# One core, a four-layer network: zero rows put into spent tiles, expert outputs written image by image with the next layer's first tokens between them

## The chip, the cores and the metric

The kernel runs on one core of a Trainium2 chip. The metric is the device time of one execution in microseconds (us); the number shown is the median of several runs. The core's engines are named as in the profile: PE (TensorE's matmuls), PEld (its weight loads), DVE (VectorE), ACT (ScalarE), POOL (GpSimd) and SP (SyncE, which here issues most of the transfers).

## The reference, cut to what matters

Two images of 64 x 64 tokens with 128 channels pass through four layers, each an attention or mixing step and a feed-forward step, in float32. The change lies between the feed-forward step of layer 2 (64 experts, each of which takes its own 8 tokens of an image) and the attention of layer 3:

```python
# layer 2, experts; x is the normalized input, 4096 tokens per image
probs = jax.nn.softmax(x @ gate_w.T + gate_b, axis=1)      # over the tokens
vals, idx = jax.lax.top_k(probs.transpose(0, 2, 1), 8)     # 8 tokens per expert
pooled = jnp.einsum('bked,bke->bed', gathered, topv)       # [2, 64, 128]
h = gelu(pooled @ weight1[e, :128] + weight1[e, 128])      # [2, 512] for each expert
out = h @ weight2[e, :512] + weight2[e, 512]               # [2, 128] for each expert
outputs = outputs.at[image, idx].add(out * topv)           # back to the chosen tokens
t = t + outputs
# layer 3, attention; x is the layer norm of t
q, k, v = x @ Wq.T + bq, x @ Wk.T + bk, x @ Wv.T + bv
t = t + softmax(q @ k.T / sqrt(256)) @ v
```

## The kernel before, in words

The tokens `x` stay in SBUF the whole time as [128 partitions, 64 blocks, 128 channels]: 32 blocks of 128 tokens per image. A framework places every tile, derives all semaphore waits, and fixes each engine's order of instructions ahead of the run: by the order in the program, with later instructions drawn forward where an engine would stand idle in its plan. Each engine then works strictly in its order. The instructions inside a conditional block are kept together: nothing of theirs is drawn ahead of the branch.

`layer2_ffn` holds the experts of layer 2. Expert rows of both images sit on 128 partitions: image 0 on 0 to 63, image 1 on 64 to 127. Its steps are these.

- `weights(1, e)` loads the first weights in 16 pieces of 1 MB (four experts each) from SP's queue into the pool `ws`, which has 12 places. The piece `e` gives its place up after the matmuls that read it.
- The gate's probabilities `pr` [128, 4096] are finished: exponential, sum, the top 8 of each row. What is not chosen becomes zero. `rest` is a tile of 16 KB per partition for this, and `prT`, in the same place afterwards, holds the transposed probabilities.
- `f2pp` sums the chosen tokens of each expert. `st1` holds the result as windows: each expert's two columns (one per image) stand at the start of a window of 34 columns, and zeros follow, so that a slice of 32 columns has only this expert's columns in its own place and zeros elsewhere. These zeros are cleared by POOL once, in L1657.
- `f2ph` (L1710) multiplies by the first weights, four column groups side by side. The result gets its bias and the gelu and is transposed.
- `st2`, four tiles like `st1` (one for each 128 of the 512 hidden units), take four places of `ws`, are cleared by POOL (L1720), and get the hidden values by four copies (L1731).
- `weights(2, e)` loads the second weights in 16 pieces of 1 MB into the same 12 places. `f2po` (L1739) multiplies by them as the pieces come, 32 column-group matmuls a piece in the records.
- The result is put in order by a small matmul (`f2sort`), and `f2y` (L1769) brings it back to the tokens: for each of eight steps `g`, four blocks of each image, alternating between the images. A block's weights are the 64 rows of its image in `pr`. Two PSUM tiles a step, out of three, and two additions to `x` (L1778) follow.

After that `layer3` makes its pool: the expert weights `ew` (SP, 512 KB), the biases `eb` (cleared by POOL, four small loads by SP) and two small cleared tiles; and it branches on `w["small"]`, a bound on the scores that was computed in layer 2. With these inputs the branch `l3_bounded` runs. `l3_qkv(b, g)` prepares a group of four blocks: statistics and reciprocal root (`l3_stats`, with a square root on ACT), normalization into `v`, four transposes and a copy into `kT`, a matmul by the combined query-key weights into `qT`, and the value bias added to `x` by POOL. The loop then goes through query blocks of 512 tokens and pairs of key blocks `k2`: scores `sc` (L2126, `scl` in the profile), exponential, and, one pair later, the values `oT` (L2085) and a running sum `acc` on DVE. Group 0 is finished before the first scores; the groups 1 to 7 of image 0 are cut into pieces, two of which follow each pair of the first query block, so that group `g` is ready at pair `2 g`.

Of the kernel before, what the change touches and what calls it, by code (L numbers as in the profile page):

```python
# [8 lines left out]
F32 = mybir.dt.float32  # L9
AF = mybir.ActivationFunctionType  # L10
ALU = mybir.AluOpType
AX = mybir.AxisListType
PSUM = bass.MemoryType.PSUM

P = 128
B = 2
S = 64
L = S * S
NC = L // P
C = 128  # L20
# [3 lines left out]
E1 = 64  # L24
FF = 512
E2 = 8
# [13 lines left out]
class Net:  # L40
# [1084 lines left out]
        yield  # L1125


    def layer2(self, kept, done, w3):
        nc, tc, ins = self.nc, self.tc, self.ins
        with tc.tile_pool(reuse_waits="tile", name="g2", bufs=1) as gp:  # L1130
            with tc.tile_pool(reuse_waits="tile", name="g2p", bufs=1, space=PSUM) as ps:
                gwT = self.load_T(gp, ps, "gwT", ins["L2_ffn_gate_w"], E1, C)
            gb = gp.tile([P, 1], F32, tag="gb", name="f2gb")
            for b in range(B):
                rows = slice(b * E1, (b + 1) * E1)
                nc.sync.dma_start(out=gb[rows], in_=column(ins["L2_ffn_gate_b"]))


            pr = gp.tile([P, L], F32, tag="pr", name="f2pr")
            mx = gp.tile([P, NC // 4], F32, tag="mx", name="f2mx")  # L1140
            mv = gp.tile([P, B * NC, 2], F32, tag="mv", name="f2mv")
            r = gp.tile([P, B * NC], F32, tag="r", name="f2r")
            gate = gwT, gb, pr, mx, mv, r
            self.layer2_attn(gate, kept, w3)
            done()
            self.layer2_ffn(gate)

    def layer2_attn(self, gate, kept, w3):

# [470 lines left out]
                pass  # L1620


    def layer2_ffn(self, gate):

# [1 line left out]
        nc, tc, ins = self.nc, self.tc, self.ins  # L1628
        NT, NR, NF = 4, E1 // 4, FF // P
        WIN = 2 * NR + 2  # L1630
        with ExitStack() as st:
            wp = st.enter_context(tc.tile_pool(reuse_waits="tile", name="f2w", bufs=1))
            ap = st.enter_context(tc.tile_pool(reuse_waits="tile", name="f2a", bufs=1))
            ps = st.enter_context(tc.tile_pool(reuse_waits="tile", name="f2p", bufs=3, space=PSUM))
            ws = st.enter_context(tc.tile_pool(reuse_waits="tile", name="f2s", bufs=12))
            _, _, pr, mx, mv, r = gate

            def weights(kind, e):
# [17 lines left out]
            st1 = wp.tile([P, NT, NR, WIN], F32, tag="st1", name="f2st1")  # L1656
# [15 lines left out]
            nc.vector.tensor_scalar(pr, pr, sm, None, ALU.mult)  # L1672
            m8 = self.small.tile([P, 8], F32, tag="m8", name="f2m8")
            nc.vector.max(m8, pr)
            rest = ap.tile([P, L], F32, tag="rest", name="f2rest")
            nc.vector.match_replace(out=rest, in_to_replace=m8, in_values=pr, imm_value=0.0)
            nc.vector.tensor_tensor(pr, pr, rest, ALU.subtract)


            prT = ap.tile([P, NC, P], F32, tag="rest", name="f2prT")  # L1680
            for g in range(NC // 4):
                pt = ps.tile([P, 4, P], F32, tag="misc", name=f"f2prT{g}")
                for i in range(4):
                    n = 4 * g + i
# [23 lines left out]
            for e in range(NR):  # L1708
                for j in range(NT):
# [4 lines left out]
                        start=(e == 0),  # L1714
                        stop=(e == NR - 1),
                    )
            st2 = []
            for c in range(NF):
                s2 = ws.tile([P, NT, NR, WIN], F32, tag="w", name=f"f2st2_{c}")
                nc.gpsimd.memset(s2, 0.0)  # L1720
                st2.append(s2)
            w2 = [weights(2, e) for e in range(NR)]
            hid = wp.tile([P, FF], F32, tag="hid", name="f2hid")
            nc.vector.tensor_tensor(hid, ph, b1, ALU.add)
# [32 lines left out]
            eo = wp.tile([P, C], F32, tag="eob", name="f2eob")  # L1757
            nc.scalar.copy(eo, pt)


            for g in range(NC // 4):
                pts = [
                    ps.tile([P, 4, C], F32, tag="misc", name=f"f2y{b}_{g}") for b in range(B)
                ]
                for i in range(4):
                    n = 4 * g + i
                    for b in range(B):
                        rows = slice(b * E1, (b + 1) * E1)
                        nc.tensor.matmul(  # L1769
                            pts[b][:, i, :],  # L1770
                            lhsT=pr[rows, n * P : (n + 1) * P],
                            rhs=eo[rows, :],
                            start=True,
                            stop=True,
                        )
                for b in range(B):
                    xs = self.x[:, b * NC + 4 * g : b * NC + 4 * g + 4, :]
                    nc.vector.tensor_tensor(xs, xs, pts[b], ALU.add)  # L1778


    def layers(self):
# [9 lines left out]
        with tc.tile_pool(reuse_waits="tile", name="l3w", bufs=1, side="right") as wp:  # L1791
# [9 lines left out]
            w["bqk"] = wp.tile([P, 1], F32, tag="bqk", name="l3bqk")  # L1801
            space = self.layer1(xT, gst, na, nb, xp, kp)
            first.close()
            self.layer2(space, kept.close, w)
            self.layer3(w)

    def layer3(self, weights):
        nc, tc, ins = self.nc, self.tc, self.ins
        G = B * NC
        with ExitStack() as st:  # L1810
            wp = st.enter_context(tc.tile_pool(reuse_waits="tile", name="l3e", bufs=1))
            weights["ones"] = wp.tile([P, 1], F32, tag="ones", name="l3ones")
            nc.vector.memset(weights["ones"], 1.0)
            weights["ew"] = self.load(
                wp, "ew", [P, E2, C], ins["L3_ffn_expert_w"].rearrange("e d c -> d e c")
            )

            eb = weights["eb"] = wp.tile([P, 4, C], F32, tag="eb", name="f3eb")
            nc.gpsimd.memset(eb, 0.0)
            for i in range(4):  # L1820
                nc.sync.dma_start(
                    out=eb[32 * i : 32 * i + E2, i, :], in_=ins["L3_ffn_expert_b"]
                )


            self.xnT = wp.tile([P, B, L], F32, tag="xnT", name="f3xnT")
            self.lg = wp.tile([P, G, E2], F32, tag="lg", name="f3lg")
            self.wt = wp.tile([P, G, E2], F32, tag="wt", name="f3wt")
            weights["pads"] = []
            for i in range(2):  # L1830
                pad = wp.tile([P, 4, 32], F32, tag=f"pad{i}", name=f"f3pad{i}")
                nc.gpsimd.memset(pad, 0.0)
                weights["pads"].append(pad)
            with tc.If(weights["small"] > 0) as fits:
                self.l3_bounded(weights)
            with fits.Else():
                self.l3_any(weights)
            self.l3_experts(weights)

    def l3_weights(self, ap, ps, w, take):  # L1840

# [172 lines left out]
    def l3_bounded(self, w):  # L2014
# [7 lines left out]
        with (  # L2022
            tc.tile_pool(reuse_waits="tile", name="l3ba", bufs=2) as ap,
            tc.tile_pool(reuse_waits="tile", name="l3bp", bufs=2, space=PSUM) as ps,
        ):
            qT = ap.tile([P, L], F32, tag="qT", name="l3qT", bufs=1)
            kTs = [ap.tile([P, L], F32, tag="kT", name=f"l3kT{b}") for b in range(B)]
            vs = [ap.tile([P, NC, C], F32, tag="v", name=f"l3v{b}") for b in range(B)]
            jobs = {}

            def piece():
# [79 lines left out]
                        for g4 in range(NB, 2 * NB - 1):  # L2111
                            jobs["bias", g4] = self.f3_bias(ap, ps, w, g4, "f3f")

            for g in range(NB):
                jobs["keys", 0, g] = keys(0, g)
            for b in range(B):
                for qb in range(NB):
# [32 lines left out]
    def l3_any(self, w):  # L2150
# [3 lines left out]
        with (  # L2154
# [1 line left out]
            tc.tile_pool(reuse_waits="tile", name="l3ap", bufs=2, space=PSUM) as ps,  # L2156
        ):
            for b in range(B):
                qT = ap.tile([P, L], F32, tag="qT", name=f"l3aqT{b}")
                kT = ap.tile([P, L], F32, tag="kT", name=f"l3akT{b}")  # L2160
                v = ap.tile([P, NC, C], F32, tag="v", name=f"l3av{b}")
                for g in range(NB):
                    for _ in self.l3_qkv(ap, ps, w, b, g, qT, kT, v, "l3a"):
                        pass
                for q in range(NC):
# [138 lines left out]
```

## Time and profile before

The median of 4 runs is 4788.3 us (4787.81 to 4790.6). The profile shows one further execution.

| | us |
|---|---|
| the profiled execution's own time | 4788.73 |
| its span, first to last instruction | 4786.9 |
| PE busy | 4471.8 (93%) |
| DVE busy | 2944.1 (62%) |
| ACT busy | 2695.8 (56%) |
| POOL busy | 945.6 (20%) |
| POOL waits for `f2ph` before it clears `st2` (one wait) | 47.9 |
| DVE waits for `f2po` (one wait) | 41.7 |
| PE waits for loads of `f2w` in `f2po` (15 waits) | 12.4 |
| PE waits for the first normalized group of layer 3 (one wait) | 5.9 |

Idle time counts only on the engine that sets the end. The long waits of POOL and DVE belong to engines that had nothing else to do in that stage; PE's short waits lie on the engine that is busy for 93% of the span. The table of shares is an average over layers of quite different kinds, so a stage has to be read by its own stretch of time: the experts of layer 2 fill about 3550 to 3682 us, and the attention of layer 3 begins there and lasts to about 4656 us.

### The profile page before, as it was taken

The page shows a single profiled execution, that of the slowest core. Times are in us where ns is not written, and L with a number is a line of the kernel's source. Part 1 is how long each engine was busy: PE and PEld are TensorE (multiplying, and loading weights), DVE is VectorE, ACT ScalarE, POOL GpSimd, SP SyncE. Part 2 cuts the span into 40 slices and gives each one's busy share as a digit, 9 for nine tenths or more (in the row PEclk, how much of TensorE's full clock was granted, in tenths as well). Part 3 has the DMA queues.
Part 4 walks back from the last instruction along what each step waited for, and adds up shares of the span by engine and source line. Part 5 has one row for each costly group of instructions (what it writes and reads, how often), then busy time and mean ns, then how long its engine had stood idle before and what let it go on. Part 6 is the DMA issues. An engine that isn't in the chain of part 4 may idle for free.

```text
span 4786.9 us, 76270 instructions
## 1 busy us (share of the span) xinstructions
PE 4471.8 (93%) x32236; PEld 1742.8 (36%) x32236; DVE 2944.1 (62%) x4850; ACT 2695.8 (56%) x3157; POOL 945.6 (20%) x848
## 2 busy tenths in 40 slices
PE   6999999998999999977899999999967999999999
PEld 3333333333333333335323223223225444444444
DVE  5676767677766767766755657555554444444447
ACT  5666565666666665545666766676731444333326
POOL 1000000000000000004455555555521000000008
PEclk8999999999999999988999999999977999999999
DMA  1000000000000000000000000000034000000001
GB/s 47 10 1 10 1 10 1 10 1 1 10 1 10 1 13 1 1 5 21 6 1 1 1 1 1 1 1 1 1 109 181 1 0 0 0 1 0 0 1 36
DMA packets 42562, 60.16 MB, mean 13 GB/s; under 512 B 4224, under 2 KB 24928, under 8 KB 41568
## 3 DMA queue, kind: packets, MB, share of 16 engines
q1 hardware_dynamic: 40912, 54.34, 3.7%
q8 instruction: 257, 4.21, 0.4%
q10 hardware_dynamic: 1296, 0.82, 0.1%
q14 instruction: 97, 0.79, 0.1%
HBM read 42.56 MB, written 4.19 MB: 10 GB/s over the span
## 4 chain that ended last, share of the span: by engine, by line
PE 76%; DVE 10%; ACT 7%; issue 3%; POOL 3%; DMA 0%; SPq 0%; ACTq 0%; POOLq 0%; DVEq 0%
PE l0o L573 16%; PE l0sc L615 16%; PE scl L2126 9%; PE oTl L2085 9%; PE l2sc L1498 5%; PE l2pos L1245 5%; PE l2av L1544 3%; PE f3ex L2235 2%; DVE l2es L1518 2%; POOL l2es L1521 2%; ACT l0es L623 2%; ACT l2es L1529 1%; DVE l0es L626 1%; PE l0pw L701 1%; PE l1p L988 1%
## 5 line engine op out<-in xcount | busy, mean ns | idle before, releaser
L626 DVE TENSOR_TENSOR l0es<-l0es,l0qe 128x1024 f32<-128x1024 f32 x1024 | 1250.3, 1228 | 529.5 <-ACT l0es L623 528.4
L623 ACT ACTIVATE l0es<-l0sc 128x1024 f32<-128x1024 f32 x1024 | 1043.3, 1024 | 603.8 <-PE l0sc L615 598.0
L573 PE MATMUL l0o<-l0es,l0v 64*33 64x512 f32 x8192 | 1071.5, 591 | 33.4 <-DVE l0es L626 17.8
L615 PE MATMUL l0sc<-l0qe,ka 64*64 64x512 f32 x8192 | 1079.2, 595 | 5.5 <-ACT l0es L623 4.9
L1529 ACT ACTIVATE l2es<-l2es 128x1024 f32<-128x1024 f32 (+3 forms) x576 | 559.1, 984 | 264.9 <-POOL l2es L1521 257.9
L1521 POOL TENSOR_TENSOR l2es<-l2es 128x1024 f32<-128x1024 f32 (+3 forms) x352 | 581.2, 1662 | 496.6 <-DVE l2es L1518 432.4
L2093 DVE TENSOR_TENSOR accl<-accl,esl 128x1024 f32<-128x1024 f32 x240 | 302.5, 1261 | 424.5 <-ACT esl L2137 421.2
L1518 DVE TENSOR_SCALAR l2es<-l2sc 128x1024 f32<-128x1024 f32 (+3 forms) x320 | 339.0, 1059 | 312.9 <-PE l2sc L1498 312.6
L2137 ACT ACTIVATE esl<-scl 128x1024 f32<-128x1024 f32 x240 | 245.6, 1023 | 485.2 <-PE scl L2126 460.1
L615 PEld LDWEIGHTS l0sc<-l0qe,ka 64*64 64x64 f32 x8192 | 298.2, 133 | 567.5 <-issue 489.7
L573 PEld LDWEIGHTS l0o<-l0es,l0v 64*33 64x33 f32 x8192 | 255.3, 108 | 648.0 <-issue 518.1
L2126 PE MATMUL scl<-l3qT,l3kT 128*128 128x512 f32 x1024 | 487.3, 595 | 0.0
L1498 PE MATMUL l2sc<-l2q,kept 32*128 32x512 f32 (+3 forms) x2304 | 390.9, 621 | 86.8 <-ACT l2es L1509 62.5
L2085 PE MATMUL oTl<-esl,l3v 128*128 128x512 f32 x960 | 451.1, 592 | 0.0
L776 POOL TENSOR_TENSOR x<-x,l0y 128x256 f32<-128x256 f32 x32 | 23.4, 731 | 1995.1 <-DVE l0y L771 1899.8
L1544 PE MATMUL l2av<-l2es,kept 128*32 128x512 f32 (+3 forms) x2304 | 310.0, 588 | 0.0
L1245 PE MATMUL l2pos<-kept 128*32 128x512 f32 x2416 | 296.5, 599 | 0.1
L2085 PEld LDWEIGHTS oTl<-esl,l3v 128*128 128x128 f32 x960 | 181.7, 190 | 225.6 <-issue 222.0
L2126 PEld LDWEIGHTS scl<-l3qT,l3kT 128*128 128x128 f32 x1024 | 188.2, 191 | 207.5 <-issue 191.3
L1509 ACT ACTIVATE l2es<-l2sc 128x1024 f32<-128x1024 f32 x224 | 226.2, 1010 | 54.3 <-PE l2sc L1498 52.9
L1498 PEld LDWEIGHTS l2sc<-l2q,kept 32*128 32x128 f32 x2304 | 116.6, 187 | 331.2 <-ACT l2es L1509 162.7
L1245 PEld LDWEIGHTS l2pos<-kept 128*32 128x32 f32 x2416 | 78.3, 111 | 174.8 <-issue 174.0
(707 smaller groups left out, 3759.7 us busy)
## 6 DMA issues: line engine op xcount, KB each, us to landing
f2w<-in_L_ffn_weight_dram SPq DMA_DIRECT2D x32, 1024.0 KB, 13.1
l0qe<-l0qe SPq DMA_DIRECT2D x8, 1024.0 KB, 6.7
x<-in_x_dram SPq DMA_DIRECT2D x8, 512.0 KB, 8.8
out_dram<-x SPq DMA_DIRECT2D x16, 256.0 KB, 2.3
kept<-in_L_attn_pos_rev_dram SPq DMA_DIRECT2D x1, 1792.0 KB, 6.3
ew<-in_L_ffn_expert_w_dram SPq DMA_DIRECT2D x1, 512.0 KB, 4.1
kept<-in_L_attn_pos_rev_dram SPq DMA_DIRECT2D x1, 256.0 KB
f2b<-in_L_ffn_weight_dram ACTq DMA_DIRECT2D x2, 128.0 KB, 2.5
```

The lines of the kernel that those rows point to most:

```text
L573: nc.tensor.matmul(o[64 * h : 64 * h + HD + 1, r, :], lhsT=v1[rows, k, 2 * pair + h, :], rhs=es[rows, h, :], start=(k == 0), stop=(k == NC ...
L615: nc.tensor.matmul(sc[64 * c : 64 * c + 64, h, :], lhsT=ka[rows, k0 : k0 + 64], rhs=qa[rows, k // (NC // 2), qs], start=True, stop=True,)
L623: nc.scalar.activation(es, sc, AF.Exp)
L626: nc.vector.tensor_tensor(es, es, ew[:, :, qs], ALU.mult)
L1245: nc.tensor.matmul(out[part], lhsT=lhsT[:, part], rhs=rhs, start=start, stop=stop)
L1498: nc.tensor.matmul(sc[:, h2, off:], lhsT=kT[hs, k * P : (k + 1) * P], rhs=q[hs, off:], start=True, stop=True,)
L1518: nc.vector.tensor_scalar(es[:, :, lo:], sc[:, :, lo:], root, None, ALU.mult)
L1521: nc.gpsimd.tensor_tensor(part, part, part, ALU.mult)
L1529: nc.scalar.activation(es[:, :, off:], es[:, :, off:], AF.Silu)
L1544: nc.tensor.matmul(avs[i][hs, off:], lhsT=v[:, k, hs], rhs=es[h // 2][:, h % 2, off:], start=(k == 0), stop=last,)
L2085: nc.tensor.matmul(oT, lhsT=vs[b][:, k, :], rhs=es[:, i, :], start=(k == 0), stop=(k == NC - 1),)
L2126: nc.tensor.matmul(sc[:, i, :], lhsT=kTs[b][:, k * P : (k + 1) * P], rhs=qT[:, qb * 512 : (qb + 1) * 512], start=True, stop=True,)
```

## The change

Three things are done.

Zero rows: the first `st2` tile is `st1` itself, whose zeros are still there and whose two columns per window are overwritten. The second and third lie in the place of `rest` and `prT`, which is enlarged from 4096 to 4352 columns for it, and only the fourth takes a place of `ws`. POOL clears three tiles and not four.

Outputs: the pools of the loads are closed after the second product. Then the eight steps run for image 0 and after that for image 1, with one PSUM tile and one addition a step.

Layer 3's beginning: between the two images `begin()` is called, which is the new `l3_begin`. It makes layer 3's pool on the other side of SBUF, with `qT`, `kT` and `v` of image 0 now in it, runs `l3_qkv(0, 0)` at once, and then does what `layer3` did ahead of the branch. The branch starts its pieces with group 1.

```diff
-            ap = st.enter_context(tc.tile_pool(reuse_waits="tile", name="f2a", bufs=1))
...
-            ws = st.enter_context(tc.tile_pool(reuse_waits="tile", name="f2s", bufs=12))
+            loads = st.enter_context(ExitStack())
+            ap = loads.enter_context(tc.tile_pool(reuse_waits="tile", name="f2a", bufs=1))
+            ws = loads.enter_context(tc.tile_pool(reuse_waits="tile", name="f2s", bufs=12))
...
-            st2 = []
-            for c in range(NF):
-                s2 = ws.tile([P, NT, NR, WIN], F32, tag="w", name=f"f2st2_{c}")
+            pair = ap.tile([P, 2, NT * WIN * NR], F32, tag="rest", name="f2st2_0")
+            last = ws.tile([P, NT * WIN * NR], F32, tag="w", name="f2st2_1")
+            st2 = [st1]
+            for s2 in (pair[:, 0], pair[:, 1], last):
                 nc.gpsimd.memset(s2, 0.0)
-                st2.append(s2)
+                st2.append(s2.rearrange("p (j r w) -> p j r w", j=NT, w=WIN))
...
-            for g in range(NC // 4):
-                pts = [
-                    ps.tile([P, 4, C], F32, tag="misc", name=f"f2y{b}_{g}") for b in range(B)
-                ]
-                for i in range(4):
-                    n = 4 * g + i
-                    for b in range(B):
-                        rows = slice(b * E1, (b + 1) * E1)
+            loads.close()
+            for b in range(B):
+                rows = slice(b * E1, (b + 1) * E1)
+                for g in range(NC // 4):
+                    pt = ps.tile([P, 4, C], F32, tag="misc", name=f"f2y{b}_{g}")
+                    for i in range(4):
+                        n = 4 * g + i
                         nc.tensor.matmul(
-                            pts[b][:, i, :],
+                            pt[:, i, :],
                             lhsT=pr[rows, n * P : (n + 1) * P],
                             rhs=eo[rows, :],
...
-                for b in range(B):
                     xs = self.x[:, b * NC + 4 * g : b * NC + 4 * g + 4, :]
-                    nc.vector.tensor_tensor(xs, xs, pts[b], ALU.add)
+                    nc.vector.tensor_tensor(xs, xs, pt, ALU.add)
+                if b == 0:
+                    begin()
...
+    def l3_begin(self, st, w):
...
+        wp = st.enter_context(tc.tile_pool(reuse_waits="tile", name="l3e", bufs=1, side="right"))
+        w["ones"] = wp.tile([P, 1], F32, tag="ones", name="l3ones")
+        nc.vector.memset(w["ones"], 1.0)
+        w["qT"] = wp.tile([P, L], F32, tag="qT", name="l3qT")
+        w["kT"] = wp.tile([P, L], F32, tag="kT", name="l3kT0")
+        w["vx"] = wp.tile([P, NC, C], F32, tag="vx", name="l3v0")
+        with (
+            tc.tile_pool(reuse_waits="tile", name="l3b", bufs=1) as ap,
+            tc.tile_pool(reuse_waits="tile", name="l3bps", bufs=2, space=PSUM) as ps,
+        ):
+            for _ in self.l3_qkv(ap, ps, w, 0, 0, w["qT"], w["kT"], w["vx"], "l3b"):
+                pass
+        w["ew"] = self.load(
+            wp, "ew", [P, E2, C], ins["L3_ffn_expert_w"].rearrange("e d c -> d e c")
+        )
...
-            qT = ap.tile([P, L], F32, tag="qT", name="l3qT", bufs=1)
-            kTs = [ap.tile([P, L], F32, tag="kT", name=f"l3kT{b}") for b in range(B)]
-            vs = [ap.tile([P, NC, C], F32, tag="v", name=f"l3v{b}") for b in range(B)]
+            qT = w["qT"]
+            kTs = [w["kT"], ap.tile([P, L], F32, tag="kT", name="l3kT1", bufs=1)]
+            vs = [w["vx"], ap.tile([P, NC, C], F32, tag="v", name="l3v1", bufs=1)]
...
-            for g in range(NB):
+            for g in range(1, NB):
                 jobs["keys", 0, g] = keys(0, g)
```

The other branch, which doesn't run here, gets the same three tiles.

## Prediction

> **What bounds the kernel now.** I began with the page. PE is busy 93% of a span of 4786.9 us, and the slices show two places where this breaks: one near 3540 to 3690 us, and the end. The diff works in the first. The table of busy time by 20 us stretches gives its stages (columns: stretch, length, busy us of PE, PEld, DVE, ACT and POOL with counts, granted clock, DMA share, GB/s):
>
> ```profile
> 3600.00:3620.00 20.00, 18.76 (x164) 9.85 (x163) 5.35 (x21) 0.00 (x0) 7.47 (x4) 1.00 0.58 216
> 3620.00:3640.00 20.00, 12.41 (x204) 8.71 (x204) 1.58 (x5) 0.63 (x1) 0.00 (x0) 0.64 1.05 386
> 3640.00:3660.00 20.00, 13.91 (x232) 9.69 (x224) 0.00 (x0) 0.00 (x0) 0.00 (x0) 0.50 1.05 386
> 3660.00:3680.00 20.00, 16.57 (x214) 13.78 (x215) 8.10 (x14) 0.27 (x1) 0.00 (x0) 0.83 0.18 67
> 3680.00:3700.00 20.00, 13.10 (x42) 6.63 (x40) 19.42 (x101) 8.40 (x13) 5.91 (x7) 0.74 0.10 28
> 3700.00:3750.00 50.00, 50.00 (x136) 23.37 (x135) 26.77 (x63) 24.57 (x32) 7.15 (x4) 1.00 0.00 1
> ```
>
> From 3620 to 3660 the DMA engines are full at 386 GB/s; from 3680 to 3700 VectorE is full while PE waits at a lowered clock; after 3700 PE is full, and it stays so (60.00 of 60.00 in each stretch to 4600). So an earlier arrival at that full stretch is an earlier end, us for us. The timeline of PE between, with the idle time ahead of each row in brackets:
>
> ```profile
> 3662.80 1.94 PE L1739 MATMUL f2po<-f2w,f2st 128*32 128x128 f32 x32 [0.78 <-DMA f2w<-in_L_ffn_weight_dram]
> 3665.41 1.66 PE L1739 MATMUL f2po<-f2w,f2st 128*32 128x128 f32 x32 [0.68 <-DMA f2w<-in_L_ffn_weight_dram]
> 3667.49 0.49 PE L1750 MATMUL f2sort<-f2eo,f2sortm 128*128 128x128 f32 x2 [0.42 <-DVE f2eo L1747]
> 3668.34 3.47 PE L1769 MATMUL f2y<-f2eob,f2pr 64*128 64x128 f32 x38 [0.35 <-ACT f2eob L1758]
> 3672.00 1.53 PE L1769 MATMUL f2y<-f2eob,f2pr 64*128 64x128 f32 x16 [0.20 <-DVE x L1778]
> ...
> 3687.75 1.15 PE L1915 MATMUL l3f_0t<-ident,l3v 128*128 128x128 f32 x4 [5.95 <-DVE l3v L172]
> 3689.62 2.07 PE L1929 MATMUL l3f_0pq<-l3kT,l3wqk 128*128 128x512 f32 x2 [0.72 <-ACT l3kT L1916]
> 3691.49 1.06 PE L1915 MATMUL l3f_1t<-ident,l3v 128*128 128x128 f32 x4
> 3692.58 4.37 PE L2126 MATMUL scl<-l3qT,l3kT 128*128 128x512 f32 x8
> ```
>
> Read here: the second expert product (f2po) ends with its last load; the outputs (f2y) go at 1.73 us per step of both images; then 10.8 us pass from the last output to the first score, because layer 3's first group is only then normalized, transposed and multiplied. VectorE's and ScalarE's rows for that chain:
>
> ```profile
> 3681.64 1.28 DVE L1778 TENSOR_TENSOR x<-x,f2y 128x512 f32<-128x512 f32 x2 [0.44 <-PE f2y L1769]
> 3682.85 0.29 DVE L1902 BATCH_NORM_STATS2 l3f_0st<-x 128x6 f32<-128x128 f32 x1
> ...
> 3684.51 1.28 ACT L98 ACT_TABLE_LOAD   x1 [16.22 <-DVE rs_v L94]
> 3685.80 0.30 ACT L98 ACTIVATE rs_s<-rs_v 128x4 f32<-128x4 f32 x2
> 3688.98 0.58 ACT L1916 COPY l3kT<-l3f_0t 128x512 f32<-128x512 f32 x1 [2.88 <-issue]
> ```
>
> **Part one, the zero rows.** Four POOL clears of 1.87 us (one row, 7.47 us for 4, starting at 3610.61) become three; the first set goes into st1, two into the probabilities' tile, one into a weight place. POOL ends at 3618.1 now and would end near 3616; what needs the clears is the VectorE copy at 3624.59, so the saved 1.87 us lies under the first product. Uncovered it would be worth that 1.87 us. The copy into st1 has to wait for the last f2ph matmul (3621.9), but the sum into hid ahead of it does so already: nothing. The two clears in the probabilities' tile wait for the last pooling matmul (3605.6) and end 3.7 us behind it, at 3609.4: nothing. Eleven places instead of eight are left for the second weights. Do loads come earlier? The queue stands still from 3583.7 to 3607.1, with twelve tiles landed, until the first f2ph matmuls give up their tiles, and that wait stays. From 3607.1 on, 20 loads of 1 MB take 2.71 us each at 386 GB/s, 54.2 us, in which the DMA rows are full. More places cannot speed up full engines: 0.
>
> **Part two, outputs image by image.** Now the matmuls alternate between images, so between partitions 0-63 and 64-127. The single records show pairs starting within 0.007 us of each other, and, where only one image has a free PSUM tile, records 0.1115 us apart (3669.336, .448, .560, .671, .783, .895). A matmul is two records, so one image's group of 4 matmuls costs 8 x 0.1115 = 0.892 us, sixteen groups 14.27, and the first record's 0.1 more, 14.4 us. Today's eight steps take 8 x 1.73 = 13.8. So the order itself loses 0.5 us: the pairing that it gives up was already held back by three PSUM tiles and two adds of 0.645 us each per step. VectorE's add (0.69) is shorter than 0.892, so PE sets the pace.
>
> The Trainium skill's page "TensorE: Matmul & The Clock Gate", section "Part 3: Packing small matmuls — row/col tiling", speaks against this edit: a weight load runs beside a matmul in flight only when the row group differs. With its load time of columns / 1.2 ns (107 ns, "LDWEIGHTS (loading the stationary operand)") as an estimate, load and matmul in turn would be 0.218 us a record, 27.9 us for the outputs, and the total 7.0 us above today's. The lone records at 0.1115 us, with loads of 188 ns under them, say that the load is hidden.
>
> **Part three, layer 3's first group between the images.** Its rows, taken at full clock: transposes 0.44 us (4 at 0.109 in later groups), the query product 0.86, on PE; on VectorE 1.2 of statistics, 0.8 for the root, 1.1 to normalize, 3.1 in all; on ScalarE the table load 1.28, root, copy 0.58, query 0.67; on POOL the bias, 1.27. All this lies beside image 1's outputs, which occupy PE for 7.1 us while VectorE is free 0.25 us in each 0.892. VectorE's total from 3669.5, 10.3 + 3.1 = 13.4 us, plus about 1 where POOL's bias add holds it (a normalization of four takes 2.06 instead of 1.11 beside one), stays under PE's 15.7. SP's issues for the expert weights and biases (0.37 + 1.37 us) and POOL's clears move ahead of image 1's adds in program order, but no output waits for either queue; what reads them comes after 4100. The added wait: the scores' PSUM tiles lie on the banks of the outputs, so the first score waits for the last adds, and with it all of PE's queue.
>
> **The sum.** Outputs start at 3668.34 in both. PE: 14.4 + 0.44 + 0.86 = 15.7, to 3684.1; last record 0.27, add 0.69, handover 0.1: 3685.15, first score (before: 3692.58). Two pairs of scores take 3.43 (before 4.37, part of it at half clock), to 3688.6. Then the next group is late: its statistics can start only behind the last add, since it stays inside the branch. Its chain was 6.7 us for group 0 (3682.85 to 3689.56); without the table load (1.28) and with less of other groups in between, 5.2 (4.6 to 5.4): keys at 3690.35. Query product 0.86 and the first values 1.72 follow, third score pair at 3693.0. Before it stood at 3699.51 with the same work behind it. Gain 6.5 us.
>
> Bounds. If PE had no hole at all, the work ahead of that pair (14.4 + 0.44 + 0.86 + 0.44 + 3.43 + 0.86 + 1.72 = 22.2) would put it at 3690.5: gain 9.0. Downward, the engines' fixed orders may make image 1's outputs wait for the root (table load plus passes, up to 2 us), and the outputs may meet a clock of 0.5 for one 3.4 us step of the clock rows (1.7 us): gain 2.8. I take 6.5, nearer the middle, as VectorE has room. The profiled execution took 4788.73 us, 0.43 above the median of 4788.3: 4782.2 for it, **4781.8** as a median.
>
> **Rivals.** (a) *The group is not drawn forward*: if the engines' fixed orders put its chain behind image 1's adds, PE's pause and its lowered clock stay, and the 0.5 us of the lone row group are lost: 4788.8. Against it: program order puts it first, and its input is ready after the first add. Chance 0.12. (b) *The places do help*: if three of the 20 loads could run in the pause before 3607, 3 x 2.71 = 8.1 us more, 4773.7. Against it: the first twelve tiles fill all places and are given up by f2ph alone. Chance 0.14. (c) *Layer 3's keys starve*, the slower side: today VectorE enters the branch 9.7 us before the first score and has groups 0 to 3 normalized by 3698; that lead is gone. PE needs a new group each 8.16 us (3703.38 to 3711.54). A group's chain is 5.2 us, plus two table loads (root and exp in turn, 2.57), plus two adds of 1.22 in VectorE's order: 10.2 if nothing overlaps. Each of the seven groups then costs 2.0 us: 4781.8 + 14.3 = 4796.1; with POOL's bias in the way (1.0) 4803. It outweighs the gain from 9.1 us per group on. Against it: chains of neighbouring groups can overlap, and VectorE's own work per group is 3.1 + 2.44 + 1 = 6.5 us of 8.16. Chance 0.14. My forecast has 0.60, its own range 4779.3 to 4785.5.
>
> **How the numbers follow.** Changes under 0.2% (9.6 us, about what a measurement of this kernel can tell from no change) lie between 4778.7 and 4797.9. The forecast, (a) and the mild end of (c) fall there: 0.72. Faster: (b) and a tail of the forecast, 0.16. Slower: the hard end of (c), 0.12. The range 4776 to 4794 leaves out most of (b) and the upper part of (c).
>
> **What would show it.** Right: f2po still ends near its last load, 20 loads in 54 us; output records 0.11 us apart in single file; transposes of group 0 among image 1's outputs; first score about 17 us behind the first output instead of 24.2; clock 1.0 through it; a hole of 1 to 2 us ahead of the second group's keys, then a full PE. Wrong: a record pitch near 0.22, repeated holes in PE up to 60 us behind the first score, or DMA work between 3584 and 3607.

## The result and the profile after

The changed kernel took 4796.01 us (median of 40 runs, 4776.97 to 4800.82) against 4787.47 us of the kernel before (60 runs, 4780.43 to 4792.45). The ratio of their means is 1.0012, with an interval of 1.0008 to 1.0017: slower by a little over a tenth of a per cent. The forecast was 4781.8, the range 4776 to 4794; the median lies above it.

The median hides that the times of the changed kernel are **of two kinds**. Eight of the 40 lie between 4776.97 and 4784.06 (median 4782.7, granted clock over the span .962 to .964), 32 between 4791.10 and 4800.82 (median 4796.5, clock .958 to .961), and nothing lies between. The times of the kernel before show no such gap (none above 2.8 us, against 7.0 here). The profiled execution is one of the shorter kind (4781.73 us, span 4779.9), so its trace alone doesn't show why the median is what it is. A second profile of the changed kernel, e7 below, caught one of the longer kind (4796.91, span 4795.1). Both are read here side by side.

First the table by stretches of time, in the shorter kind (stretch, length, busy us of PE, PEld, DVE, ACT, POOL with counts, granted clock, DMA share, GB/s):

```profile
3640.00:3660.00 20.00, 14.12 (x236) 10.19 (x240) 0.00 (x0) 0.00 (x0) 0.00 (x0) 0.50 1.03 380
3660.00:3680.00 20.00, 18.35 (x179) 15.57 (x172) 11.61 (x33) 3.03 (x5) 2.09 (x4) 0.92 0.12 34
3680.00:3700.00 20.00, 17.33 (x57) 9.05 (x56) 19.14 (x87) 9.29 (x13) 4.77 (x4) 0.91 0.00 0
3700.00:3750.00 50.00, 48.37 (x127) 21.85 (x127) 25.11 (x58) 27.75 (x33) 6.88 (x4) 1.00 0.00 0
```

and in the longer kind:

```profile
3660.00:3680.00 20.00, 17.77 (x147) 16.41 (x140) 7.25 (x21) 1.75 (x3) 0.82 (x3) 0.59 0.20 63
3680.00:3700.00 20.00, 20.00 (x68) 14.71 (x67) 9.55 (x37) 1.49 (x4) 1.27 (x1) 0.52 0.00 1
3700.00:3750.00 50.00, 46.11 (x121) 21.16 (x120) 33.91 (x117) 31.24 (x38) 11.64 (x7) 0.97 0.00 1
```

The stretch to look at is the second of the longer kind: PE is busy for the whole 20.00 us and yet has only a clock of 0.52. Before the change the same stretch had 13.10 us of work at 0.74, so a low clock went with a pause. Here it goes with none.

The timeline of PE says which instructions these are. The shorter kind:

```profile
3664.05 0.49 PE L1757 MATMUL f2sort<-f2eo,f2sortm 128*128 128x128 f32 x2 [0.42 <-DVE l3ones L1821]
3664.90 10.20 PE L1774 MATMUL f2y<-f2eob,f2pr 64*128 64x128 f32 x92 [0.35 <-ACT f2eob L1765]
3675.29 0.33 PE L1932 MATMUL l3b_0t<-ident,l3v 128*128 128x128 f32 x1 [0.20 <-DVE l3v L172]
...
3678.09 1.12 PE L1946 MATMUL l3b_0pq<-l3kT,l3wqk 128*128 128x512 f32 x2
3679.15 2.94 PE L1774 MATMUL f2y<-f2eob,f2pr 64*128 64x128 f32 x24
3682.07 2.81 PE L2143 MATMUL scl<-l3qT,l3kT 128*128 128x512 f32 x6
3687.55 0.99 PE L1932 MATMUL l3f_1t<-ident,l3v 128*128 128x128 f32 x3 [2.67 <-DVE l3v L172]
...
3692.93 1.88 PE L2143 MATMUL scl<-l3qT,l3kT 128*128 128x512 f32 x4
...
3704.32 1.98 PE L2102 MATMUL oTl<-esl,l3v 128*128 128x512 f32 x4 [1.34 <-ACT esl L2154]
```

and the longer:

```profile
3666.66 17.67 PE L1774 MATMUL f2y<-f2eob,f2pr 64*128 64x128 f32 x92 [0.35 <-ACT f2eob L1765]
3684.26 0.47 PE L1932 MATMUL l3b_0t<-ident,l3v 128*128 128x128 f32 x1
...
3689.13 2.07 PE L1946 MATMUL l3b_0pq<-l3kT,l3wqk 128*128 128x512 f32 x2
3691.13 5.49 PE L1774 MATMUL f2y<-f2eob,f2pr 64*128 64x128 f32 x24
3696.55 4.14 PE L2143 MATMUL scl<-l3qT,l3kT 128*128 128x512 f32 x6
```

The same 92 records take 10.20 us (0.111 each) in the one and 17.67 in the other; the last 24 take 2.94 and 5.49. The first score stands 17.2 us behind the first output in the shorter kind (3682.07 less 3664.90) and 29.9 us in the longer: 12.7 of the 13.8 us between the two medians.

What comes behind the first score is late too, by less. In the shorter kind PE waits 2.67 us for the second group, and its chain on VectorE and ScalarE reads:

```profile
3682.13 0.69 DVE L1782 TENSOR_TENSOR x<-x,f2y 128x512 f32<-128x512 f32 x1 [0.20 <-PE f2y L1774]
...
3686.20 0.18 DVE L100 RECIPROCAL rs_r<-rs_s 128x4 f32<-128x4 f32 x2
...
3687.15 1.12 DVE L172 TENSOR_SCALAR l3v<-x,l3f_1mv,l3f_1r 128x128 f32<-128x128 f32 x4
```

```profile
3690.50 0.59 ACT L1933 COPY l3kT<-l3f_1t 128x512 f32<-128x512 f32 x1 [2.50 <-PE l3f_1t L1932]
```

From the end of the last addition (3682.82) to the end of that copy (3691.09) 8.3 us pass.

A measure that leaves out when the stage began is used below: **the rest**, the span less the start of the first output. It is 4786.9 - 3668.34 = 1118.6 us before the change, 1115.0 in the shorter kind and 1128.4 in the longer.

### The profile page after: what moved, and what is told of

It is laid out like the page before. It is cut to its first block, busy times and chain, and to the rows that moved or that the text cites. A ratio compares the mean times of both kernels' runs of the same rounds, so it can differ in the third digit from the quotient of the medians.

```text
span 4779.9 us, 76267 instructions
## 1 busy us (share of the span) xinstructions
PE 4470.4 (94%) x32236; PEld 1744.4 (36%) x32236; DVE 2944.1 (62%) x4850; ACT 2702.6 (57%) x3161; POOL 945.3 (20%) x847
## 4 chain that ended last, share of the span: by engine, by line
PE 74%; DVE 11%; ACT 7%; POOL 3%; issue 3%; DMA 1%; SPq 0%; POOLq 0%; DVEq 0%; ACTq 0%
PE l0o L573 16%; PE l0sc L615 15%; PE scl L2143 9%; PE oTl L2102 9%; PE l2sc L1498 5%; PE l2pos L1245 5%; PE l2av L1544 3%; PE f3ex L2250 2%; DVE l2es L1518 2%; POOL l2es L1521 2%; ACT l0es L623 2%; ACT l2es L1529 1%; DVE l0es L626 1%; PE l0pw L701 1%; PE l1p L988 1%
```

## The experiments

The theory at this point: 64 rows of the array alone (one image's outputs) do not raise a lowered clock, though the two images' 64 rows side by side do, and so the order by images lets the clock stay at 0.5 where it happens to be there at the start. The rival: the lowered clock is an accident of layer 3's earlier beginning, or of the zero rows' loads, and the order of the outputs has no part in it.

**e1: the changed kernel unchanged**, in another set of runs.

> The changed kernel unaltered, to see an execution of its common, longer kind: 31 of its 40 times lie between 4791 and 4801 us, 9 between 4777 and 4784, and the profile shown is one of the 9. Theory one, the clock: the outputs of one image use only 64 rows of the array, and such matmuls don't raise a granted clock of 0.5; where the clock is at 0.5 when the outputs begin, all 128 records go at 0.223 us and not 0.1115, 28.6 us in place of 14.3, so the two kinds should lie 14 us apart and the mean clock 0.003. A longer execution's trace should show records 0.22 us apart and the clock at 0.5 through the outputs. Theory two, layer 3's keys: the records stay 0.11 us apart, and some 14 us of holes lie in PE in the 60 us behind the first score. Theory three, something ahead of 3540 us: the outputs begin 14 us later than in the other trace.

Measured: 4792.98 us (4781.76 to 4797.76, 10 runs), ratio 1.0012 (1.0002 to 1.0021). Three lie at 4781.76 to 4784.48, seven at 4791.29 to 4797.76. The two kinds are the kernel's own. The profile is of the shorter kind again.

**e2: the zero rows alone**, in the kernel before.

```diff
-            for c in range(NF):
-                s2 = ws.tile([P, NT, NR, WIN], F32, tag="w", name=f"f2st2_{c}")
+            pair = ap.tile([P, 2, NT * WIN * NR], F32, tag="rest", name="f2st2_0")
+            last = ws.tile([P, NT * WIN * NR], F32, tag="w", name="f2st2_1")
+            st2 = [st1]
+            for s2 in (pair[:, 0], pair[:, 1], last):
```

> The kernel before with the new places of the zero rows alone: outputs and layer 3 as before. All theories: no change, within 2 us of the kernel before, one kind of times, since the loads fill the DMA engines from 3607 us to their end in both. If the places do help, up to 8 us less.

Measured: 4785.92 us (4782.92 to 4787.77, 10 runs), ratio 1.0 (0.9991 to 1.001); one kind of times. No worth of the zero rows can be told from nothing, and 8 us are out. Its profile shows by chance what the old order does with a lowered clock. The outputs begin at 0.5 (stretches, columns as above):

```profile
3664.00:3668.00 4.00, 4.00 (x30) 4.00 (x32) 1.28 (x2) 0.00 (x0) 0.00 (x0) 0.51 0.00 0
3668.00:3680.00 12.00, 9.62 (x103) 8.28 (x99) 8.98 (x16) 0.00 (x0) 0.82 (x3) 1.00 0.01 2
```

Four microseconds of outputs, most of them in pairs and without a pause, and the clock is 1.0. This is the one trace in which the outputs began at 0.5.

**e3: the outputs image by image alone**, in the kernel before.

```diff
-            for g in range(NC // 4):
-                pts = [
+            for b in range(B):
+                rows = slice(b * E1, (b + 1) * E1)
+                for g in range(NC // 4):
+                    pt = ps.tile([P, 4, C], F32, tag="misc", name=f"f2y{b}_{g}")
```

> The kernel before with outputs image by image alone, nothing between them and zero rows as before. Theory one, the clock: two kinds of times 14 us apart, most executions about 4788 + 14 = 4802 us, the rest near 4789. Theory two, layer 3's keys: 0.5 us more than before, one kind, since layer 3 begins as before.

Measured: 4797.14 us (4780.15 to 4798.78, 10 runs), ratio 1.0017 (1.0007 to 1.0026): seven at 4794.99 to 4798.78, two near 4788.6, one at 4780.15. The profile is of the longer kind:

```profile
3665.90 25.40 PE L1767 MATMUL f2y<-f2eob,f2pr 64*128 64x128 f32 x128 [0.35 <-ACT f2eob L1758]
3696.86 1.15 PE L1912 MATMUL l3f_0t<-ident,l3v 128*128 128x128 f32 x4 [5.56 <-DVE l3v L172]
```

All 128 records of the outputs without a pause take 25.40 us, where 14.4 were reckoned: the first 15 ran at a clock of 1.0, the others about 0.21 us apart, so the longer kind lies lower than the 4802 expected. Neither the zero rows nor layer 3's beginning is in this kernel: the order of the outputs alone brings the longer kind.

**e4: the changed order on all 128 rows.** The result is copied into two tiles, each with one image's rows and zeros in the other's; every output matmul then works on all rows, with the same sums.

```diff
-            eo = wp.tile([P, C], F32, tag="eob", name="f2eob")
-            nc.scalar.copy(eo, pt)
+            for b in range(B):
+                rows = slice(b * E1, (b + 1) * E1)
+                nc.scalar.copy(eos[rows, b, :], pt[rows])
...
-                            lhsT=pr[rows, n * P : (n + 1) * P],
-                            rhs=eo[rows, :],
+                            lhsT=pr[:, n * P : (n + 1) * P],
+                            rhs=eos[:, b, :],
```

> The changed kernel with each output matmul on all 128 rows; the other image's rows of the moving side are zero, so the sums are the same, and the records have the same number and, at full clock, the same 0.11 us pitch. Theory one, if the clock goes by the rows in use: the clock rises within 7 us of the first output, and the times are of one kind, about 4783 us (5 below the kernel before). Theory one, if it goes by something else than rows: still two kinds, most about 4796. Theory two, layer 3's keys: as the changed kernel, two kinds, most about 4796.

Measured: 4782.23 us (4776.19 to 4785.33, 10 runs), ratio 0.9988 (0.9979 to 0.9998), one kind. The rows in use are the only thing that differs in PE's work, and the longer kind is gone. (Two copies in place of one also let the first output start 0.05 us later, after 0.40 us of idle time and not 0.35.)

```profile
3667.32 10.54 PE L1777 MATMUL f2y<-f2eob,f2pr 128*128 128x128 f32 x92 [0.40 <-ACT f2eob L1768]
```

The pitch is the same 0.11 us (10.54 / 92): a record on all rows is no slower. Since as many records come in a step as with 64 rows, it isn't the number of matmuls that makes the difference. e12 below is a second profile of it.

**e5: layer 3's beginning with the outputs in pairs**, as before the change, `begin()` after the fourth of the eight steps.

```diff
-            for b in range(B):
-                rows = slice(b * E1, (b + 1) * E1)
-                for g in range(NC // 4):
+            for g in range(NC // 4):
...
-                if b == 0:
+                if g == 3:
                     begin()
```

> The changed kernel with the outputs in the old order, both images in turn at each of eight steps, and layer 3's beginning called after the fourth step. Theory one, the clock and the rows: with both halves of the array in use the clock rises soon after the first output, so the times are of one kind, about 4782 us (4 to 5 below the kernel before, as the kernel with all rows). If image order itself, and not the rows, makes the two kinds: the same 4782. If the beginning between the outputs makes them: two kinds, most about 4796.

Measured: 4782.76 us (4776.95 to 4784.39, 11 runs), ratio 0.9990 (0.9981 to 0.9999), one kind; the rest 1115.4. So without the lone rows the other parts are a gain of about 4 us (0.5 to 9 by the interval), and the change would have been a small step forward.

Pairs don't guard the clock in every case, though. In e5's profile it falls at 3678.3, behind the step in which the transposes break up the outputs, and stays at 0.5 for 10.2 us, through these rows:

```profile
3679.54 2.07 PE L1949 MATMUL l3b_0pq<-l3kT,l3wqk 128*128 128x512 f32 x2
3681.54 2.93 PE L1776 MATMUL f2y<-f2eob,f2pr 64*128 64x128 f32 x20
```

The same query product takes 1.12 us in the changed kernel's shorter kind. So e5's rest has a stretch of low clock in it, and how often that happens in its other executions isn't known.

**e6: e5 with the second group drawn forward too**, to see what the hole ahead of its keys is worth.

```diff
-            for _ in self.l3_qkv(ap, ps, w, 0, 0, w["qT"], w["kT"], w["vx"], "l3b"):
-                pass
+            for g in range(2):
+                for _ in self.l3_qkv(ap, ps, w, 0, g, w["qT"], w["kT"], w["vx"], "l3b"):
+                    pass
```

> As e5_pairs, with layer 3's groups 0 and 1 both prepared there, so that the branch starts with group 2. The trace of the changed kernel has a hole of 2.67 us in PE behind the first scores, because group 1's keys come late (kT of group 1 at 3691.1, predicted 3690.35 less the 3.4 us by which that trace's outputs began earlier), and later holes of 1.34 and 0.29 us. If the lateness of group 1 is what took half of the predicted gain: these holes are gone and the time is 3 us below e5_pairs. If PE's outputs are only pushed back by the second group's transposes: the same time as e5_pairs.

Measured: 4783.18 us (4780.96 to 4788.14, 11 runs), ratio 0.9992 (0.9983 to 1.0001): no different from e5. It has two holes, as e5 has (0.56 and 2.50 us there):

```profile
3686.89 0.75 PE L1936 MATMUL l3f_2t<-ident,l3v 128*128 128x128 f32 x3 [0.58 <-DVE l3v L172]
...
3703.56 2.86 PE L2106 MATMUL oTl<-esl,l3v 128*128 128x512 f32 x4 [2.50 <-ACT esl L2158]
```

ScalarE explains it:

```profile
3699.68 1.28 ACT L98 ACT_TABLE_LOAD   x1 [3.75 <-DVE rs_v L94]
3700.97 0.20 ACT L98 ACTIVATE rs_s<-rs_v 128x4 f32<-128x4 f32 x1
3701.19 1.28 ACT L2158 ACT_TABLE_LOAD   x1
3702.49 1.02 ACT L2158 ACTIVATE esl<-scl 128x1024 f32<-128x1024 f32 x1
```

A root for a later group stands in ScalarE's order ahead of the exponential that PE's next values need. It waits for VectorE, and two table loads of 1.28 us lie around it. The hole belongs to that order; drawing one more group forward only sets it 2 us earlier (38.4 us behind the first output, 40.4 in e5).

**e7: the changed kernel, profiled again**, for the longer kind.

> The changed kernel unaltered once more, to see its longer kind in a trace. Theory one, the clock: where the time is above 4790 us, the clock is at 0.5 during the outputs and their records are 0.21 to 0.22 us apart; the outputs take some 25 us and not 17. Theory two, layer 3's keys: records 0.11 us apart and holes in PE behind the first score.

Measured: 4796.91 us, the longer kind, whose rows are shown with the result. Its clock by stretches:

```profile
3664.00:3668.50 4.50, 3.72 (x50) 3.18 (x43) 0.95 (x3) 1.55 (x2) 0.82 (x3) 0.88 0.39 107
3668.50:3680.00 11.50, 11.50 (x59) 11.50 (x59) 6.30 (x19) 0.21 (x1) 0.00 (x0) 0.50 0.03 7
3680.00:3690.00 10.00, 10.00 (x38) 7.96 (x37) 4.83 (x13) 0.59 (x1) 1.27 (x1) 0.50 0.01 2
3690.00:3699.00 9.00, 9.00 (x29) 6.37 (x28) 3.72 (x17) 0.75 (x2) 0.00 (x0) 0.50 0.00 0
```

The clock is 1.0 for one step as the outputs begin, falls at 3668.5, and stays at 0.5 for 30.7 us though PE has no pause while the outputs last. It rises only when the scores, on all 128 rows, have come. So the clock isn't at 0.5 at the start, as the theory had it; it is lost one step in.

**e8 and e11: lone rows four times over.** Each output matmul of the changed kernel is issued four times with the same result, so that single file on 64 rows lasts some 60 us. e8 is one profiled execution, e11 the same kernel with times.

```diff
-                        nc.tensor.matmul(
+                        for _ in range(4):
+                            nc.tensor.matmul(
```

> The changed kernel with each output matmul issued four times with the same result, so that 64-row matmuls of one image run alone for long. Theory one: the clock, if at 0.5, stays there through all of them, or falls there if it was at 1.0, though PE has no pause: some 100 us for the outputs. If 64-row matmuls alone do raise the clock after some steps: under 70 us, with the clock at 1.0 for most of it.

> The kernel of e8 once more, for its times: each output matmul four times over, in single file on 64 rows. If such matmuls hold a clock of 1.0 but never raise one of 0.5, the times fall into two kinds as the changed kernel's do, but four times as far apart: about 4824 where the clock holds, and about 4824 + 55 = 4879 where it falls at the start (512 records of 0.112 us at 0.223). If they only raise it late, after some 30 us, the longer kind lies near 4824 + 13 = 4837. If the clock's fall has nothing to do with the rows, and it is any work of this length that is let down once, the times are one kind near 4824.

Measured: e8 4824.35 us; e11 4825.82, 4877.00, 4878.08 and 4879.27. e8's profile, with the clock at 1.0 from 3664.0 for 68 us:

```profile
3668.00:3700.00 32.00, 32.00 (x277) 30.83 (x277) 8.75 (x26) 1.48 (x3) 1.26 (x1) 1.00 0.01 2
3700.00:3726.00 26.00, 26.00 (x228) 25.46 (x227) 5.61 (x9) 0.00 (x0) 0.00 (x0) 1.00 0.01 1
```

e11's profile (4878.08 us):

```profile
3668.10:3700.00 31.90, 31.90 (x153) 31.90 (x152) 6.67 (x23) 0.20 (x1) 1.26 (x1) 0.50 0.02 6
3700.00:3780.00 80.00, 80.00 (x358) 76.46 (x358) 8.83 (x22) 1.27 (x2) 0.00 (x0) 0.50 0.00 1
```

The same program, the same work, PE full in both: a clock of 1.0 in the one for as long as the outputs last, 0.5 in the other for 112.6 us. The two kinds are 53 us apart, nearly four times the 13.8 of the changed kernel (55): the price grows with the outputs' work and isn't a fixed accident. So lone rows **hold** a clock of 1.0 and do **not raise** one of 0.5. The group of full-array work between the images in e11 (four transposes and the query product, 3.2 us in all) didn't raise it either:

```profile
3719.71 1.11 PE L1933 MATMUL l3b_0t<-ident,l3v 128*128 128x128 f32 x4
3722.76 2.07 PE L1947 MATMUL l3b_0pq<-l3kT,l3wqk 128*128 128x512 f32 x2
```

**e10: layer 3's beginning called after all outputs**, in pairs.

```diff
-                if b == 0:
-                    begin()
+            begin()
```

> The changed kernel with the outputs in the old order of pairs and layer 3's beginning behind all of them: part three's place alone is undone. If the place between the outputs is what brings e5's 3.8 us, nearly all of it goes: 4786 to 4787, one kind of times, the first score some 23 to 24 us behind the first output. If the gain comes from the beginning's new place in the program alone (the expert weights' issues, the tiles made ahead, group 0 outside the branch), it stays near 4783.

Measured: 4779.52 us (4775.30 to 4783.47, 10 runs), ratio 0.9984 (0.9974 to 0.9994), one kind. The expectation's first case, that nearly all of the gain goes, didn't come; its second did. It has the lowest median of all versions, below both kernels; the rest is 1112.5, which is 6.1 less than before. PE's timeline shows why:

```profile
3678.83 1.16 PE L1776 MATMUL f2y<-f2eob,f2pr 64*128 64x128 f32 x10 [0.20 <-DVE x L1785]
3679.92 0.66 PE L1934 MATMUL l3b_0t<-ident,l3v 128*128 128x128 f32 x4
3681.25 1.13 PE L1948 MATMUL l3b_0pq<-l3kT,l3wqk 128*128 128x512 f32 x2 [0.68 <-ACT l3kT L1935]
3683.20 2.81 PE L2145 MATMUL scl<-l3qT,l3kT 128*128 128x512 f32 x6 [0.82 <-ACT rs_s L98]
...
3690.31 1.88 PE L2145 MATMUL scl<-l3qT,l3kT 128*128 128x512 f32 x4
...
3702.59 3.65 PE L2104 MATMUL oTl<-esl,l3v 128*128 128x512 f32 x4 [2.24 <-ACT esl L2156]
```

The framework draws the group's normalization among the additions by itself, and PE transposes right behind the last output. No output is held up by a transpose, so the last addition ends 14.5 us behind the first output, and not 16.9 as in e6 (pairs with the group between them, clock 1.0 throughout) or 17.9 as in the changed kernel, and the second group starts that much sooner: the third score pair stands 23.7 us behind the first output, against 28.0. The clock stays at 1.0 from 3665.0 to 3702.6, unlike in e5, so part of e10's lead over e5 in the rest (2.9 us) can be the clock's. The hole by ScalarE's order (2.24 us) is there as in e6.

**e12: e4's kernel, profiled again.**

> The kernel of e4 for another profile: outputs one by one on all 128 rows. If a full array raises the clock within one step, the clock is 1.0 through the outputs apart from at most one step of 3.4 us, and the first score comes 17 to 19 us behind the first output, wherever the clock stood when they began. If e4 only happened to start warm, a fall to 0.5 as in e7 can show here too, with the first score near 30 us behind.

Measured: 4780.81 us, the first score 16.1 us behind the first output (3682.05 less 3665.98), clock 1.00 from 3668 to 3682. With e4's ten runs that is eleven executions on all rows without one of the longer kind, where the lone rows had 39 of 50 (32 of 40, and 7 of 10 in e1). The outputs began with the clock just risen both times; one that begins on all rows at 0.5 was not caught, so for the zeros it is the times, not a trace, that show the clock is kept.

**e13: e10 with the first group back in the branch**; of part three only the tiles, loads and clears stay early.

```diff
-            for _ in self.l3_qkv(ap, ps, w, 0, 0, w["qT"], w["kT"], w["vx"], "l3b"):
-                pass
...
-            for g in range(1, NB):
+            for g in range(NB):
                 jobs["keys", 0, g] = keys(0, g)
```

> The kernel of e10 with layer 3's first group back in the branch, so that of part three only the earlier tiles, loads and clears are left. If e10's 7.4 us come from the group standing ahead of the branch, where the engines' fixed orders can mix it with the outputs wherever begin() is called, all of it goes: 4786 to 4788, the first transposes near 19 us behind the first output with a pause of about 6 us ahead of them, the first score some 24 us behind. If they come from the earlier tiles and loads, it stays near 4780.

Measured: 4786.62 us (4780.56 to 4790.66, 10 runs), ratio 1.0 (0.999 to 1.001); the rest 1119.0. PE's pause is back:

```profile
3685.17 1.16 PE L1928 MATMUL l3f_0t<-ident,l3v 128*128 128x128 f32 x4 [6.10 <-DVE l3v L172]
```

The gain of part three comes from taking the group out of the branch (the rest is 1119.0 with it inside, 1112.5 outside; the intervals of the two ratios just touch). None can be seen from the loads and tiles, or from the place of the call.

The rest, in one table (us):

| kernel | outputs | first group of layer 3 | span | first output | rest |
|---|---|---|---|---|---|
| before | pairs | in the branch | 4786.9 | 3668.34 | 1118.6 |
| e2 (outputs began at 0.5) | pairs | in the branch | 4785.1 | 3664.00 | 1121.1 |
| e13 | pairs | in the branch | 4784.6 | 3665.61 | 1119.0 |
| e10 | pairs | ahead, called last | 4779.1 | 3666.59 | 1112.5 |
| e5 | pairs | ahead, called between | 4781.9 | 3666.47 | 1115.4 |
| e6 | pairs | two groups ahead, called between | 4779.7 | 3665.18 | 1114.5 |
| e4, e12 | single, all rows | ahead, called between | 4780.8, 4779.0 | 3667.32, 3665.98 | 1113.5, 1113.0 |
| after, e1, shorter kind | single, 64 rows | ahead, called between | 4779.9, 4780.3 | 3664.90, 3666.05 | 1115.0, 1114.2 |
| after, longer kind (e7) | single, 64 rows | ahead, called between | 4795.1 | 3666.66 | 1128.4 |
| e3, longer kind | single, 64 rows | in the branch | 4795.4 | 3665.90 | 1129.5 |

## Why the prediction was wrong, point by point

**Part one, the zero rows**: right. Zero was forecast, e2 measured a ratio of 1.0 (0.9991 to 1.001). The queue still stands for 23.2 us ahead of the 20 loads (23.1 before), and they still take 56.7 us from first to last packet (56.8 before; 54.2 reckoned), so the second rival (places that help) is out.

**Part two, outputs image by image**: here the prediction failed. "16 groups, 14.27 us" multiplied a duration by a count and took the clock along unasked: the six lone records at 0.1115 us stood in a stretch whose clock had risen 1.7 us ahead of the first output and stayed at 1.0 under the pairs. At that clock the figure is right (0.111 in the shorter kind). At 0.5 the records stand 0.21 apart, and nothing in that stretch could say whether lone rows keep a clock of 1.0 or what they do to one of 0.5. The bound that was given for it, "a clock of 0.5 for one 3.4 us step (1.7 us)", supposes that outputs raise the clock within a step; e3, e7 and e11 show that lone rows set no such end. The term was mis-sized by 12.7 us in the longer kind, and 39 of 50 executions were of that kind. "A record pitch near 0.22" was named as a sign of error, for another reason (loads that aren't hidden); the pitch came, and the reason is the clock.

The Trainium skill's page "TensorE: Matmul & The Clock Gate", section "What's actually happening", says that one busy window of about 3.4 us releases the throttle. By that rule the lowered clock would cost at most a few microseconds here. The pairs of e2 agree with it; the lone rows don't (nor do the outputs and the query product at 0.5 in e5, where PE was full from 3678.3 to 3681.7): in e11 PE was busy without a pause through 33 steps of 3.41 us at 0.5 (every stretch at one clock in these traces lasts a multiple of 3.41). The measurement decides, and it adds a condition that the sentence hasn't got: whether half the rows or all of them are in use counts (e4 against the changed kernel).

**Part three, the first group between the images**: the mechanism was right, the size too large. First score 17 us behind the first output forecast, 17.2 in the shorter kind; transposes among image 1's outputs, as said; a hole of 1 to 2 us, 2.67 in fact. The sum's step "keys at 3690.35", 5.2 us behind the last addition, was the short one: it took 8.3 us, because VectorE's fixed order takes the roots of groups 1 and 2 together and PE's order puts the last transpose behind two records of scores, which ran at a clock of 0.5 (3687.1 to 3690.5). The third score pair stood 28.0 us behind the first output, where 24.7 was forecast and 31.2 was measured before. A second hole (1.34 us) followed by ScalarE's table loads. In all the shorter kind gains 3.6 us of rest and not 6.5. In e10, where the outputs aren't interrupted, the same part gains 6.1.

**Rivals.** (a) fell: the group was drawn forward; e13, with the group in the branch and the outputs in pairs, is near to what (a) describes, 4786.6. (b) fell with e2. (c), keys that starve: one hole or two of 1.3 to 2.7 us, not one for each of seven groups; PE is full from 3710 on in the shorter kind. That (c) named 4796.1, the time measured, is a coincidence: 12.7 of the 13.8 us lie ahead of the first score, where it put none.

**The gap that the rivals left.** All of them took the outputs as full-clock work. The rival that was missing starts with what the prediction had on the table: f2po runs at a clock of 0.50 for most of its time (the stretch 3640 to 3660), the clock is 1.0 only from just ahead of the outputs, and the edit takes away the pairs that kept it there.

What stays open is why the clock holds in some executions and falls in others one step into the outputs. The traces do differ in one thing: how far ahead of the first output the clock rose, which also sets how much of that first step is f2po's work and how much is outputs (us, from the granted clock and PE's rows):

| profile (outputs single, 64 rows) | clock rises ahead of the first output | f2po in that step | outputs in that step | one step later |
|---|---|---|---|---|
| after | 1.74 | 0.48 | 1.67 | stays 1.0 |
| e1 | 1.79 | 0.52 | 1.62 | stays 1.0 |
| e8 | 1.74 | 0.47 | 1.68 | stays 1.0 |
| e3 | 1.64 | 0.37 | 1.77 | falls |
| e7 | 1.58 | 0.32 | 1.83 | falls |
| e11 | 1.57 | 0.31 | 1.84 | falls |

With pairs the clock stayed in e10 at 1.58, in e6 at 1.62 and in e13 at 1.64, on the side where lone rows lost it. Three profiles on each side, 0.10 us apart, are a hint and no proof: no run varied this distance alone. On all rows e4 and e12 stood at 1.77 and 1.76, so their traces don't test the other side; their eleven times do, as far as they fell on it.

Open too is what exactly raises a clock of 0.5. Pairs without a pause did within a step (e2); in e5 pairs with a pause of 0.46 us behind them did not. Whether e4's zeros would raise it from the first output on wasn't seen.

## What to carry to other kernels

A duration is read together with the clock it was taken at, and before matmuls are moved to fewer rows of the array, it has to be asked what raises the clock there and what keeps it: here full rows with zeros in them cost nothing (0.11 us a record in both) and took the two kinds of times away. When times fall into two groups, one profile shows only one of them, and a second profile of the same kernel comes before any experiment. Work that should run beside the end of a stage has only to stand outside the branch; called last it was no worse here (4779.5) than set between by hand (4782.8; the intervals overlap).

## What was not expected of the hardware

With PE busy in every microsecond the granted clock stayed at 0.5 for 112.6 us under matmuls on 64 rows, with 3.2 us of full-array work among them (e11), and at 1.0 for the 59 us that the same ones took in e8. The program was the same; what differed was how the first step went.
